# Graph layers on one core: the first load goes first, the parameters come later by GpSimd's queue, two key buffers, and a new order of all steps

## The chip, the cores and the metric

The kernel runs on one core of one Trainium2 chip. A core has TensorE (PE, matrix products; its weight loads are shown apart as PEld), VectorE (DVE), ScalarE (ACT), GpSimd (POOL) and SyncE (SP). Each works through its own list of instructions in order; semaphores let one wait for another. SP, ACT and POOL also issue DMA transfers, each from its own list, so that a DMA stands in line behind whatever its engine waits for. Time is device microseconds of one launch, the median of several runs.

## The reference, cut to what matters

Sixteen graphs (batches) of 1024 nodes with 64 channels go through four layers. Each is followed by an addition of its input and a norm over the channels. `adj` is 16 x 1024 x 1024 float32, with some ten entries in a row.

```python
# layer 0
x = ln(x + adj @ (x @ W0) + bias0)
# layer 1: Chebyshev, three products with adj
z1 = adj @ x; z2 = 2 * adj @ z1 - x; z3 = 2 * adj @ z2 - z1
x = ln(x + x @ th[0] + z1 @ th[1] + z2 @ th[2] + z3 @ th[3])
# layer 2: per node a weighted sum of quantiles (0.25, 0.5, 0.75) over its neighbours
nb = thinned(adj > 0, nodemask)          # rows with over 10 neighbours lose some
agg = weighted_quantiles(x, nb)          # a sort over a ragged list, for each channel
x = ln(x + (relu((x + agg) @ W1 + b1) @ W2 + b2) * nodemask)
# layer 3: batch norm over all batches, normalised Laplacian, leaky relu
x = ln(x + leaky((I - D^.5 A D^-.5) @ (bn(x) @ W3 + b3)))
```

## The kernel before

All 16 batches go through one software pipeline, and a last phase (lines 1640 to 1740) finishes layer 3, since its statistics run over all batches. Lines 1090 to 1640 hold a slow path for other data, which does not run here.

A batch's work is cut into nine parts, each a Python generator that gives up control at its `yield`s. The pieces between are called steps:

- `rows in` (11 steps): the x load and the first two adjacency tiles (`load`); eight tiles of 128 rows (`tile0` to `tile7`); a transpose of x; the first product with adj (`sum`). A tile's step takes the sign on ACT into `key` (L534), eight transposes on PE and two copies on ACT (`transposed`, L489, L490), the product with `keyband` on DVE (L536), eight maxima (L539), three rounds of maxima for the list (L543, L546), and issues the load of the tile after the next.
- `layers` (13): layer 0 (`part`, L570, L581), its norm (squares L440, root L443, reciprocal L445, products L450), then three hops with adj (L464) with a transpose after each, theta's product (`out`, L619), a norm, the store of the rows to DRAM for the gathers (`rows`) and x in three pieces (`parts`, L500, L502).
- `lists` (15): who is removed; nodes ordered by their number of neighbours, on PE (`before`, L724 to L728) and by eight one-hot tiles (`at0` to `at7`, L742); the ids (L765) with a comparison with caps (L775).
- `fetch` (15): 70 indirect DMAs from POOL (L803), each followed by a memset that only takes time (L806).
- `heads` (10): the gathered rows of the classes 0, 1 and 5 (24, 11 and 8 slots of 1, 4 and 3 blocks of nodes) go into the tile `home` with ACT (L875), after `dead` on DVE (L827 to L846).
- `sorts` (141): for each class a step of weights (L904), sorting steps on DVE between the tiles `home` and `away` (L907), and two or three steps of sums, products on ACT (L923) and sums on PE (L924). Class 0 has steps 0 to 84, class 1 85 to 122, class 5 123 to 140, of which 139 and 140 are sums.
- `ends` (5): the perceptron of layer 2 and its norm. `back` (11): nodes into their first order, by eight one-hot tiles (`order0` to `order7`, L988). `third` (5): adj is loaded back and multiplied once more.

No scheduler orders these: `tc.manual_schedule()` keeps the program's order. Each step has a moment in `WHEN`; batch b's step stands at b x 120 + moment, and the steps of all batches are sorted by that and written out one after the other. The moments are thus no times, only an order, the same for all engines. What an engine executes is this order, cut to its own instructions, each with its waits. Four or five batches are in work at once.

A tile name with `bufs` has so many buffers; a new tile waits for the last reader of the buffer that it gets. `key` has one, `f_a` (adjacency tiles), `at16` and `home` have two, `away` one, PSUM bank `end` one. A pool that is closed gives its memory to the next, which then waits.

Before the pipeline come the parameters (L257 to L415): loads on SP and ACT, the mask's transpose (L278), theta, W0, W2 and the biases centred on DVE, mostly in a pool `f_first` of its own that is closed ahead of the pipeline's pools. Then come keyband and columns (L1050, L1052), the memsets of the gather tiles on POOL (L1061), and the sorted steps. The loop at the end of the pipeline:

```python
        for _, b, name, u, part in sorted(parts, key=lambda p: p[0]):
            next(part)
```

## Time and profile before

| | us |
|---|---|
| median of 3 runs (2221.63 to 2226.77) | 2222.99 |
| the profiled execution, timed | 2229.29 |
| its span, first to last instruction | 2227.4 |
| first gather starts | 121.6 |
| ids of batch 0 to ids of batch 15 | 119.3 to 1940.6 |
| last phase starts | about 2147 |
| mean granted TensorE clock | 0.871 |

The profiled execution is 6.3 us above the median. The page gives busy time for each engine, slices of the span, the chain of work that ended last, groups of equal instructions with what ended the idle time before them, and DMA issues. A wait reads "engine, tile and line that waited <- what released it: total us, times, longest". A line of the timeline reads "start, length, engine, line, operation, tiles, count [idle before <- releaser]"; ACTq, SPq and POOLq are the queues' own instructions, DMA issues among them.

Where the time goes by stretches, busy us of each:

| stretch, us | DVE | ACT | PE | POOL |
|---|---|---|---|---|
| 0 to 121.6 | 83.3 | 51.6 | 85.2 | 5.0 |
| 121.6 to 243.4 | 95.1 | 62.5 | 81.0 | 109.7 |
| 243.4 to 365.1 | 111.3 | 89.4 | 96.8 | 108.1 |
| 974.0 to 1095.8 | 109.5 | 87.2 | 97.4 | 101.8 |
| 1948.1 to 2060.0 | 83.6 | 78.2 | 60.9 | 100.0 |
| 2060.0 to 2147.0 | 35.0 | 39.5 | 54.8 | 5.8 |
| 2147.0 to 2227.4 | 49.2 | 26.5 | 30.5 | 32.7 |

### The profile page before, as it was taken

The numbers are of one execution on the slowest core, as the hardware profiler recorded it, in microseconds if no ns is written. First come the engines' busy times: TensorE is split into PE (matmuls) and PEld (weight loads), VectorE is DVE, ScalarE is ACT, GpSimd is POOL, SyncE is SP. The second block draws the span as 40 slices with busy tenths as digits, with TensorE's granted clock in tenths as the row PEclk, the third lists the DMA queues.
The fourth block names the chain that finished last, engine by engine and source line by source line (L and its number), as shares of the span: only waits on it lengthen the run. The fifth ranks groups of instructions, "written<-read, shape, count | busy, mean of one in ns | idle before, by whom it ended". The sixth has DMA issues, their size and how long they took to land. (4 is left out here: it accounts for less than half of the span.)

```text
span 2227.4 us, 35713 instructions
## 1 busy us (share of the span) xinstructions
PE 1671.2 (75%) x9926; PEld 935.9 (42%) x9926; DVE 1864.1 (84%) x5687; ACT 1484.5 (67%) x5397; POOL 1734.7 (78%) x2279
## 2 busy tenths in 40 slices
PE   4876788878788778878788778878787877755653
PEld 3443444444445344444435344444444443333333
DVE  7658989889898989989898989999998988677536
ACT  3544767768686767768685767768686766675523
POOL 0078989899989989978787978889888979888014
PEclk9988889889899999989899998989998988876675
DMA  4444253533435353533535353533435352231226
GB/s 148 167 112 130 72 186 92 167 97 109 155 87 177 92 194 82 173 98 99 161 87 174 91 193 83 174 96 118 145 85 181 97 183 75 57 105 26 82 81 158
DMA packets 130481, 272.42 MB, mean 122 GB/s; under 512 B 77025, under 2 KB 77281, under 8 KB 120033
## 3 DMA queue, kind: packets, MB, share of 16 engines
q1 hardware_dynamic: 57536, 218.90, 27.2%
q0 software_dynamic: 35840, 37.92, 10.4%
q10 hardware_dynamic: 36896, 13.23, 2.4%
q8 instruction: 80, 1.31, 0.2%
q14 instruction: 129, 1.05, 0.2%
HBM read 185.89 MB, written 84.07 MB: 121 GB/s over the span
## 5 line engine op out<-in xcount | busy, mean ns | idle before, releaser
L803 POOL DMA_INDIRECT got<-rows,ids x1072 | 1139.7, 1063 | 186.0 <-issue 125.0
L806 POOL MEMSET rest<- 128x384 f32 x1120 | 509.4, 455 | 0.6
L464 PE MATMUL ps_l<-f_adj_t,f_t 128*64 128x512 f32 x1536 | 359.0, 622 | 35.5 <-ACT f_t L603 35.5
L875 ACT ACTIVATE home<-got,big 128x64 f32<-128x64 f32 x1344 | 329.9, 334 | 0.0
L907 DVE TENSOR_TENSOR away<-home 128x768 f32<-128x768 f32 (+9 forms) x416 | 228.9, 572 | 43.6 <-PE ps_xt L924 34.5
L924 PE MATMUL ps_xt<-home,quarter 128*128 128x256 f32 (+2 forms) x672 | 199.1, 404 | 65.0 <-ACT home L923 58.5
L923 ACT ACTIVATE home<-home,wts 128x64 f32<-128x64 f32 x896 | 226.8, 336 | 2.2 <-DVE home L907 2.0
L464 PEld LDWEIGHTS ps_l<-f_adj_t,f_t 128*64 128x64 f32 x1536 | 110.3, 142 | 250.7 <-issue 207.3
L539 DVE MAX8 cand<-key 128x8 f16<-128x128 f16 x1024 | 210.6, 278 | 4.4
L803 POOL DMA_INDIRECT extra<-rows,more x48 | 50.8, 1058 | 177.0 <-ACT row L780 116.1
L534 ACT ACTIVATE key<-f_a 128x1024 f16<-128x1024 f32 x128 | 135.0, 1055 | 59.2 <-DVE cand L539 42.1
L489 PE MATMUL ps_turn<-cf,f_a 128*128 128x128 f32 x1024 | 149.2, 293 | 31.2 <-ACT f_adj_t L490 18.1
L907 DVE TENSOR_TENSOR home<-away,home 128x128 f32<-128x128 f32 (+5 forms) x352 | 166.4, 473 | 6.2
L924 PEld LDWEIGHTS ps_xt<-home,quarter 128*128 128x128 f32 x672 | 110.5, 214 | 139.6 <-ACT home L923 139.5
L490 ACT COPY f_adj_t<-ps_turn 128x512 f32<-128x512 f32 x256 | 135.7, 582 | 39.3 <-PE ps_turn L489 39.3
L489 PEld LDWEIGHTS ps_turn<-cf,f_a 128*128 128x128 f32 x1024 | 120.4, 149 | 79.8 <-issue 47.6
L907 DVE TENSOR_TENSOR home<-away 128x64 f32<-128x64 f32 (+7 forms) x304 | 149.7, 510 | 1.1
L536 DVE TENSOR_TENSOR key<-key,keyband 128x1024 f16<-128x1024 f16 x128 | 87.6, 685 | 53.8 <-ACT key L534 53.8
L464 PE MATMUL ps_end<-f_adj_t,f_u 128*64 128x512 f32 x512 | 124.2, 641 | 8.9 <-ACT f_u L1015 8.9
L924 PE MATMUL ps_xt<-away,quarter 128*128 128x64 f32 (+1 forms) x448 | 94.9, 340 | 47.4 <-ACT away L923 46.8
L510 PE MATMUL ps_end<-at,f_h 128*64 128x512 f16 x256 | 62.3, 464 | 85.6 <-DVE at L988 85.5
L907 DVE TENSOR_TENSOR home<-home 128x64 f32<-128x64 f32 (+7 forms) x240 | 120.1, 500 | 7.2
(248 smaller groups left out, 3472.4 us busy)
## 6 DMA issues: line engine op xcount, KB each, us to landing
f_a<-in_adj_dram SPq DMA_DIRECT2D x128, 512.0 KB, 3.6
adj<-f_adj_t SPq DMA_DIRECT2D x16, 4096.0 KB
f_adj_t<-adj SPq DMA_DIRECT2D x64, 1024.0 KB, 22.2
got<-rows,ids POOLq DMA_INDIRECT x1072
rows<-xr ACTq DMA_DIRECT2D x16, 264.0 KB, 17.1
f_x<-in_x_dram ACTq DMA_DIRECT2D x16, 256.0 KB, 5.3
x_d<-f_x SPq DMA_DIRECT2D x16, 256.0 KB
z_d<-f_ht SPq DMA_DIRECT2D x16, 256.0 KB
```

What stands on the lines that cost most here:

```text
L464: nc.tensor.matmul(ps[h * C : (h + 1) * C, :], lhsT=v[:, j, :], rhs=pairs[:, j, h], start=(j == 0), stop=(j == NK - 1),)
L489: nc.tensor.transpose(pt[:, j * P : (j + 1) * P], a[:, (4 * g + j) * P : (4 * g + j + 1) * P], ident)
L490: nc.scalar.copy(adj_t[:, 4 * g : 4 * g + 4, i * P : (i + 1) * P], pt.rearrange("p (j n) -> p j n", n=P))
L534: nc.scalar.activation(flat_key, a, AF.Sign)
L536: nc.vector.tensor_tensor(out=flat_key, in0=flat_key, in1=keyband[:, off : off + N], op=ALU.mult)
L539: nc.vector.max(out=cand[:, i, j * 8 : j * 8 + 8], in_=key[:, j, :])
L803: nc.gpsimd.indirect_dma_start(out=w[0], out_offset=None, in_=rows[:, :], in_offset=bass.IndirectOffsetOnAxis(ap=w[1], axis=0))
L806: nc.gpsimd.memset(rest, 0.0)
L875: nc.scalar.activation(home[:, s + 1, k, :], got[:, s, k, 0:C], AF.Identity, bias=big_dead[:, s, k : k + 1], scale=1.0,)
L907: nc.vector.tensor_tensor(out=at(ho, r1 if is_max else r0, *run), in0=at(ha, r0, *run), in1=at(hb, r1, *run), op=ALU.max if is_max else AL ...
L923: nc.scalar.mul(t[:, k, :], t[:, k, :], wts[:, i, k : k + 1])
L924: nc.tensor.matmul(total, lhsT=quarter, rhs=flat(t), start=False, stop=(i == nr - 1))
```

## The change

It does four things.

- The parameters' loads leave SP's and ACT's queues and are issued by POOL, from the new function `given`, called right after batch 0's `load` step. Their working tiles are two `f_ht` buffers in place of the pool `f_first`. POOL's three memsets of the gather tiles come behind them. Keyband moves from SP's queue to ACT's, ahead of x; the columns follow x.
- Their preparation becomes a generator, `prepared`, in three pieces that run after batch 0's steps `rows in` 8 (`tile7`), `rows in` 10 (`sum`) and `layers` 1 (`square`). The arithmetic is the same, but for one subtraction that nobody used.
- `key` has two buffers.
- All moments in `WHEN` are new. In steady state this places, for example, `out` (L624 in after) between two pieces of class 5's sums and ahead of `tile6`'s transposes on PE, `perc` behind the next batch's `sum`, and the first two tiles' loads and the reload of adj some 20 to 55 earlier.

Lines behind L520 stand 5 lower in the file after; `hop2`, `norm` and `transposed` stand 74 higher.

```diff
+KEYS = 2
+SETUP = (("rows in", 8), ("rows in", 10), ("layers", 1))
...
 WHEN = {
-    "rows in": (-237, -232.5, -224.8, -221.8, -214.5, -211.4, -205.5, -203.1, -200.2, -196.4, -192.2),
-    "layers": (-156, -124.5, -120.4, -111.8, -102.1, -98.2, -94.1, -87.1, -85, -81.1, -76.5, -76.3, -70),
-    "lists": (-133.4, -133.4, -125.8, -125.8, -99.2, -69.7, -69.6, -67.8, -65.7, -63, -59.4, -58.3, -55.8, -40.9, -4.9),
-    "fetch": (-27, -9.9, -9.3, 4.7, 4.7, 4.7, 4.7, 4.7, 4.7, 26.1, 28.6, 42.7, 55.6, 64.2, 64.2),
-    "heads": (25.6, 34.3, 34.8, 84.7, 97.5, 97.5, 104.6, 135.7, 140.2, 142.2),
+    "rows in": (-291.1, -231, -226.2, -221.4, -216.1, -211.1, -203.2, -202.1, -200.7, -195.1, -189.8),
+    "layers": (-161.4, -122.7, -116.3, -107.2, -103.4, -100.5, -94.9, -86.6, -82.5, -82.1, -77.1, -70.1, -68),
+    "lists": (-136.1, -134.1, -134, -126.8, -94.1, -66.3, -64.9, -63.8, -53.4, -53.2, -50.1, -43.3, -41.9, -15.3, -4.7),
+    "fetch": (-2.9, -2.9, -0.1, 7.1, 18.4, 20.7, 29.9, 29.9, 29.9, 29.9, 29.9, 30.5, 30.6, 36, 48.7),
+    "heads": (24.2, 36.5, 36.6, 89.8, 104.8, 107.1, 109.7, 129.4, 134.3, 140.7),
     "sorts": (
...
-        146.7, 147, 147, 147, 147, 147, 148.1, 148.2, 154.7, 155.6, 155.6, 155.6, 156.2, 156.9, 157.4, 158.8,
+        156, 156, 156, 156, 157.9, 158.8,
     ),
-    "ends": (159.7, 161.1, 161.2, 173.5, 185.2),
-    "back": (137.4, 189.4, 195.6, 202.6, 202.7, 206.9, 209.5, 215.7, 220.2, 220.2, 224.2),
-    "third": (212.3, 228.2, 241.9, 249.6, 264.9),
+    "ends": (164.6, 169.7, 171.2, 175.2, 199.2),
+    "back": (140.7, 166.9, 200.2, 202.8, 208.3, 208.3, 212.8, 215, 217, 221.7, 226.5),
+    "third": (190.8, 233.1, 244.7, 252.9, 270.2),
...
+    def given(pw):
+        one, two = (pw.tile([P, 512], F32, name="f_ht", bufs=2) for _ in range(2))
...
+        for h in range(2):
+            nc.gpsimd.dma_start(out=w0_c[h * C : (h + 1) * C, 0, :], in_=w0)
+        nc.gpsimd.dma_start(out=left[:, 0, :], in_=bias0.rearrange("(o c) -> o c", o=1).to_broadcast([3, C]))
+        nc.gpsimd.dma_start(out=left[:, 1, :], in_=b2.rearrange("(o c) -> o c", o=1).to_broadcast([3, C]))
+        nc.gpsimd.dma_start(out=mask_u, in_=nodemask.rearrange("b (k p) -> (b k) p", p=P))
+        nc.gpsimd.dma_start(out=th, in_=theta.rearrange("k i o -> i k o"))
+        nc.gpsimd.dma_start(out=w2_s, in_=w2)
+        for h in range(2):
+            nc.gpsimd.dma_start(out=w1_2[h * C : (h + 1) * C], in_=w1)
+        nc.gpsimd.dma_start(out=b1_s, in_=b1.rearrange("(h o) -> h o", o=1))
+        return th, thp, mean, w0_c, left, mine, term
...
+    def prepared(th, thp, mean, w0_c, left, mine, term):
+        halves = [slice(h * C, (h + 1) * C) for h in range(2)]
+        centred(mean, w0_c)
...
+        nc.vector.tensor_copy(out=biases, in_=mine)
+        yield
+        nc.vector.tensor_copy(out=mask_f, in_=mask_u)
+        pm = bank("end")
+        nc.tensor.transpose(pm[:, 0:P], mask_f, ident)
+        nc.vector.tensor_copy(out=mask_t, in_=pm[:, 0:P])
+        nc.vector.tensor_copy(out=earlier, in_=earlier_f)
...
+        centred(mean, thp)
+        thf = bank("end").rearrange("p (k c) -> p k c", c=C)[:, 0:4]
+        nc.tensor.matmul(thf, lhsT=but_last, rhs=thp, start=True, stop=True)
+        for hp in halves:
+            nc.vector.tensor_copy(out=th_c[hp, :, hp], in_=thf[hp])
+        yield
+        nc.vector.tensor_copy(out=w2_c[:, 0, :], in_=w2_s)
+        centred(mean, w2_c)
+        nc.vector.tensor_scalar(out=node, in0=own, scalar1=-1.0, scalar2=None, op0=ALU.add)
+        nc.scalar.mul(quarter, ident, 0.25)
+        nc.scalar.mul(minus_i, ident, -1.0)
+        yield
...
-            key = pa.tile([P, NK, P], F16, name="key")
+            key = pa.tile([P, NK, P], F16, name="key", bufs=KEYS)
...
-        nc.sync.dma_start(out=keyband, in_=ch_d[:, 5 * P : 5 * P + BAND])
+        nc.scalar.dma_start(out=keyband, in_=ch_d[:, 5 * P : 5 * P + BAND])
...
+        def setup():
+            nc.scalar.dma_start(out=columns, in_=ch_d[:, 5 * P + BAND : 6 * P + BAND + N])
+            todo = prepared(*given(pw))
+            for ns, _, _, ks in CLASSES:
+                if any(WHOLE[k] < ns for k in ks):
+                    nc.gpsimd.memset(gots[ks[0]], 0.0)
+            nc.vector.tensor_copy(out=rec[:, :, OTHERS], in_=own)
+            for u in SETUP:
+                then[0, *u] = lambda: next(todo)
...
+        then = {(0, "rows in", 0): setup}
         for _, b, name, u, part in sorted(parts, key=lambda p: p[0]):
             next(part)
+            if (b, name, u) in then:
+                then[b, name, u]()
```

## The prediction

> **What bounds the kernel now.** I read the busy times first, then five windows of 126 us, then VectorE's waits, then the timeline of the first 125 us and of one cycle.

> ```profile
> span 2227.4 us, 35713 instructions
> PE 1671.2 (75%) x9926; PEld 935.9 (42%) x9926; DVE 1864.1 (84%) x5687; ACT 1484.5 (67%) x5397; POOL 1734.7 (78%) x2279
> ...
> 804.00:930.00 126.00, 99.42 (x623) 55.61 (x620) 113.88 (x355) 92.52 (x339) 109.35 (x144) 0.93 0.45 136
> ...
> L765 ACT CAST ids<-ps_l x16: 312/318/318, 119.3 to 1940.6; 128x184 int32<-128x184 f32 x16
> ```

> VectorE (DVE) is busiest, with 113.9 of a cycle's 126 us, and GpSimd (POOL) follows with 109.4. The window's columns are length, PE, PE weight loads, DVE, ACT, POOL. The list of ids is made once a batch: 15 steps from 119.3 to 1940.6 are 121.4 us each. In single rows it is made for batch 1 at 209.3 and for batch 14 at 1825.42, so the 13 cycles between take 124.3 each. A batch's 70 gathers need some 70 x (1063 + 455 + 160) ns = 117.5 us of POOL (mean gather, mean memset, the pause that the rows show), so POOL is not the bound; it waits for ids and rows. What separates DVE from a full cycle is this (300 to 1800 us, 12 cycles):

> ```profile
> DVE key L536 <- ACT key L534: 21.5, 12, 2.4
> DVE x_mid L500 <- ACT f_h L450: 20.8, 10, 2.1
> DVE at L988 <- PE ps_end L510: 18.7, 28, 1.9
> DVE away L907 <- PE ps_xt L924: 12.2, 12, 1.0
> DVE n_r L445 <- ACT n_d L443: 4.2, 10, 0.4
> DVE x_mid L500 <- issue: 4.2, 2, 2.1
> ```

> Per cycle: 1.8 for the sign key, 2.1 for x_mid, 1.6 for order tiles, 1.0 for the first sort step, 0.4 for a root: 6.9 us. The rest of the idle time is pauses of some 0.05 us. So at most 6.9 us a cycle can be won by another order. The start is the other place:

> ```profile
> 15.59 0.33 SPq L1050 DMA_DIRECT2D keyband<-in_ch_dram  x1
> ...
> 15.96 24.99 SPq L481 DMA_DIRECT2D f_a<-in_adj_dram  x8
> ...
> 21.25 1.06 ACT L534 ACTIVATE key<-f_a 128x1024 f16<-128x1024 f32 x1 [16.36 <-DMA f_a<-in_adj_dram]
> ...
> 47.57 9.05 PE L464 MATMUL ps_l<-f_adj_t,f_x 128*64 128x512 f32 x32
> ...
> 61.72 1.28 ACT L443 ACT_TABLE_LOAD   x1
> ```

> The first adjacency load is issued at 15.96, when the parameters are done (their pool's memory is used again), and its sign runs at 21.25.

> **The start, step by step.** The load now stands second on SP, behind cf (issued at 0.76), so at some 1.2 us; with the same 5.3 us to its sign this runs near 6.5, say 6.8: 14.4 us earlier. Keyband and x go by ACT's own queue, in front of the sign, and have landed by then as x does before. Eight DVE tiles take 3.70 each before (23.06 to 26.76) and have no gap, so a second key buffer gives nothing here; they end 14.4 earlier.

> Then part is given back. In times of before, less 14.4: DVE ends tile 7 at 51.95; the first piece of preparation (L443 to L467) repeats rows that span 11.07 to 15.52, with the centres 4.6 us: 56.5, while PE's hop runs to 56.6. But in PE's new order the mask transpose and theta's product (L472, L487) stand between hop and layer 0's product (L575). Mask cast, transpose 0.48, copy 0.29, then DVE's casts and eight theta steps, 2.5: the product starts at 60.1, takes 1.2, and layer 0's product ends at 63.7 instead of 58.9. DVE goes on with theta's copies (0.9), the whole lists (51.95 to 60.4 before: 8.5), w2's centring (1.0) and only then reaches the reciprocal of layer 0: 72.0 instead of 63.5. So 8.5 is lost and 5.9 remains. In batch 0's layers the out product (L624) now stands ahead of tile 6's transposes on PE, so that tile's copies, the next sign and the squares of the second norm come later: the rows above give 2.3, and 0.4 for the hop behind. The lists of batch 1 now start before the cap comparison that waited 2.0 us. Net: -5.9 + 2.7 - 2.0 = -5 us. From 178 us on DVE is saturated and passes this on. Bounds: -14.4 if all is hidden, +3 if POOL's loads are late.

> Ten small loads move from ACT's and SP's queues to POOL, ahead of its three memsets (4.79 us). At 1.06 us each (a gather's row) they are issued by 12 us and the memsets by 17. Needed first is w0 at 37.5. The first gather comes past 115. Cover: 20 us; without it a us late is a us lost. A row shows what POOL's memsets do to DVE copies:

> ```profile
> 0.75 4.79 POOL L1061 MEMSET got<- 128x1518 f32 x3 [0.29 <-POOLq L1751]
> ...
> 3.41 2.18 DVE L379 COPY w_c<-w_s 128x64 f32<-128x64 f32 x1 [1.41 <-DMA w_s<-in_L_gnn_W_dram]
> ```

> That copy ends with the memset (5.59 against 5.54). In after the memsets fall on tiles, which are tensor_tensor and max, not copies, so I charge 0.

> [...]

> **The cycle, step by step.** I laid the after order of each engine beside the rows of one cycle and asked which wait must remain.
> - Sign key, 1.8: with two buffers the sign waits for no max. From `dead5`, for which ACT waits, ACT has 13.3 us of work to `dead0` and DVE 22.3: a lead of 9. From there to tile 5's sign ACT has 21.7 and DVE 16.4: 5.3 of the lead are used. 0 (high 1.8).
> - First sort step, 1.0: it must wait until the old away buffer is read. Before, 21 products of class 5 (5.1 us) run after the last step and DVE hides 3.9 of it in tile 6. Now PE's order is three sums, out product, tile 6's transposes, four sums; ACT's is nine products, sign 6, tile 6's copies, twelve products. Chain after the last step: 2.2 + 0.3 + 3.7 (L619) + 1.05 + 0.6 + 2.2 + 1.1 = 11.1; less 0.5 for ranks ready early. DVE has two tiles and the weights between, 7.6. So 3.0 (low 2.8; high 5.4 with ACT as late as the 2.4 us seen at the key).
> - x_mid behind eight ACT products in one step: unchanged, 2.1.
> - Order tiles: spread between sort steps, 1.6 becomes 0 (high 1.6). Root: ten sort steps instead of six cover it, 0 (high 0.4).
> - New: `perc` now stands behind the next batch's hop on PE (7.7 mean, 8.4 in this cycle), then 2.4 and ACT's eight, 1.8; DVE's addition comes 9 us after the root: 0.5 (0 to 3).
> - New: class 1 starts when its last 16 home copies (3.9) are done, behind ten products (2.4); lists cover all but 1.0 (0 to 3).

> Sum 3.0 + 2.1 + 0.5 + 1.0 = 6.6 against 6.9: -0.3, times 13 is -4. All low ends give 4.9, -2.0 a cycle; all high ones 17.3, but a wait gives ACT and PE a lead for the next, so I stop at 9.5: +2.6 a cycle.

> **The end.** Ids of batch 14 start the last two rounds of gathers; beside DVE's cycle they come 0 to 2 us later, and in the last batch class 5's start stands earlier among the steps: 0 in all (+-5).

> Sum: -5 - 4 = -9: span 2218.4, and 2220.3 timed, as the profiled execution took 2229.29. That is 6.3 above the median of the runs, 2222.99; put against the median the forecast is 2223 - 9 = 2214.

> **Rivals.**
> 1. *The sums wait* (slower). First sort step and class 1 both meet their high ends; the place is PE's out product ahead of the four sums. For it: ACT is busy 92 of 126 us and its 1.8 us lateness at the key is exactly in this stretch. Against: ACT has no max to wait for. Price: +2.4 + 2.0 - 0.3 = +4.1, eased to +2 a cycle, 13 x 2 - 5 = +21: 2244. It decides from +0.8 a cycle.
> 2. *The order works as drawn*: only x_mid stays, -4.8 a cycle. -62 - 5: some 2156; POOL's 117.5 is then just not reached. For it: no wait but the 2.1 is forced by data alone. Against: the 11.1 us chain.
> 3. *The first load does not do what it says*: all 14.4 is given back, since layer 0 needs what was moved behind it; the cycle gives -4: 2219.

> **How the numbers follow.** Chances: forecast 0.50 (own range 2200 to 2226), first rival 0.24, second 0.16, third 0.10. About 0.2%, 4.4 us, is what a measurement of this kernel can tell from no change. Of the forecast's 0.50 I count 0.35 faster, 0.13 same, 0.02 slower; of the third 0.05, 0.03, 0.02. Faster 0.56, same 0.16, slower 0.28. The range cuts the fast end of rival 2 and takes in most of rival 1: 2182 to 2242.

> **What would show it.** First sign near 6.8 us; layer 0's reciprocal at 57 to 58; first gather near 118. In mid cycle a wait of some 3 us at the first sort step for ps_xt, none for the key, and cycles of ids at 124 us. It is wrong if the first sort step waits over 4 us, if DVE waits for got (gathers late), if cycles fall below 121, or if the reciprocal already comes at 50.

## The result and the profile after

| | before | after |
|---|---|---|
| median, us (4 runs each) | 2222.31 (2220.84 to 2226.77) | 2285.98 (2284.47 to 2287.2) |
| ratio after to before, 95% interval | | 1.028 (1.0261 to 1.0299) |
| span of the profiled execution | 2227.4 | 2285.2 |
| mean granted TensorE clock | 0.871 | 0.831 |

The kernel became slower by 2.8%; forecast were 2214 us and a range up to 2242. The ids of each batch split the 57.8 us between the spans:

| stretch | before | after | difference |
|---|---|---|---|
| start to the ids of batch 1 | 209.3 | 200.2 | -9.1 |
| 13 cycles, ids of batch 1 to ids of batch 14 | 1616.1 | 1677.6 | +61.5 |
| ids of batch 14 to ids of batch 15 | 115.2 | 112.3 | -2.9 |
| ids of batch 15 to the end | 286.8 | 295.1 | +8.3 |

So the start won time, the end gave 5.4 back in all, and the cycle lost 4.7 us, 13 times. The page of after begins:

```profile
span 2285.2 us, 35621 instructions
...
PE 1753.8 (77%) x9926; PEld 989.9 (43%) x9926; DVE 1861.3 (81%) x5686; ACT 1486.0 (65%) x5397; POOL 1749.6 (77%) x2289
```

VectorE's work is the same (1861.3 against 1864.1). TensorE runs the same 9926 products and needs 82.6 us more for them (1753.8 against 1671.2): its instructions became longer. VectorE's waits of after, 300 to 1800 us, which holds 11 to 12 cycles:

```profile
DVE away L912 <- PE ps_xt L929: 46.6, 11, 4.5
DVE x_mid L505 <- ACT f_h L376: 25.0, 12, 2.1
DVE f_h L966 <- issue: 21.6, 8, 3.1
DVE n_r L371 <- ACT n_d L369: 13.6, 20, 1.2
DVE f_h L966 <- ACT f_h L965: 9.9, 4, 2.9
DVE at L747 <- PE ps_px L515: 6.7, 11, 0.7
DVE key L541 <- ACT key L539: 4.1, 9, 1.6
```

The key's wait is nearly gone, but per cycle the first sort step now waits 4.2 us, the perceptron's addition f_h 2.7, x_mid 2.1, the root 1.2, a one-hot tile 0.6, the key 0.3: 11.1 in place of before's 6.6 (both over the ten cycles from the fourth to the fourteenth ids, waits of over 0.25 us each). Nearly all but x_mid lies in one stretch of some 35 us, from the last sums of class 5 to f_h. TensorE's rows there, in one cycle of after:

```profile
1311.25 0.59 PE L929 MATMUL ps_xt<-away,quarter 128*128 128x192 f32 x2 [1.93 <-DVE wts L909]
1311.97 1.73 PE L929 MATMUL ps_xt<-home,quarter 128*128 128x192 f32 x4
1313.49 4.91 PE L624 MATMUL ps_l<-th_c,f_ct 128*128 128x128 f32 x32
1318.24 1.04 PE L415 MATMUL ps_turn<-cf,f_a 128*128 128x128 f32 x8
1320.72 0.59 PE L929 MATMUL ps_xt<-away,quarter 128*128 128x192 f32 x2 [1.44 <-ACT away L928]
...
1329.37 0.94 PE L402 MATMUL ps_xt<-cf,f_ht 128*128 128x128 f32 x4 [2.10 <-ACT f_ht L937]
...
1332.99 8.78 PE L390 MATMUL ps_l<-f_adj_t,f_x 128*64 128x512 f32 x32
```

The out product takes 4.91 us and the hop 8.78. The same two in the same stretch of before:

```profile
1299.07 4.13 PE L619 MATMUL ps_l<-th_c,f_ct 128*128 128x128 f32 x32
...
1309.92 7.09 PE L464 MATMUL ps_l<-f_adj_t,f_x 128*64 128x512 f32 x32
```

Over the ten cycles from the fourth ids to the fourteenth, the out product takes 4.80 on average in after and 4.01 in before, the hop 8.75 and 7.67. The prediction took 3.7 for the out product, as rows of before with the full clock have it (those that start at 98.67 and 921.21 us). The windows of the stretch in after show why; they are cut on the raster of 3.41 us on which the clock's changes lie (last section; columns as in the prediction: length, PE, weight loads, DVE, ACT, POOL, granted clock, DMA share, GB/s):

```profile
1305.71:1309.12 3.41, 3.41 (x18) 1.08 (x14) 3.27 (x6) 3.41 (x12) 3.08 (x5) 1.00 0.10 20
1309.12:1312.54 3.42, 1.37 (x6) 0.60 (x4) 3.28 (x11) 3.42 (x13) 3.09 (x5) 1.00 0.55 176
1312.54:1315.95 3.41, 3.29 (x15) 3.27 (x15) 3.20 (x15) 1.04 (x2) 3.08 (x5) 0.50 0.19 22
1315.95:1319.36 3.41, 3.33 (x30) 3.09 (x29) 2.50 (x14) 0.48 (x2) 3.08 (x5) 1.00 0.19 19
1319.36:1322.78 3.42, 1.78 (x6) 0.89 (x6) 0.01 (x1) 3.42 (x15) 3.09 (x6) 1.00 0.12 21
1322.78:1326.19 3.41, 3.33 (x14) 3.24 (x15) 3.29 (x10) 2.14 (x5) 3.08 (x5) 0.50 0.11 20
1326.19:1329.60 3.41, 1.31 (x12) 1.12 (x11) 3.23 (x10) 3.19 (x19) 3.08 (x5) 1.00 0.89 356
1329.60:1333.02 3.42, 2.75 (x10) 0.84 (x8) 3.32 (x7) 1.27 (x3) 3.09 (x5) 0.50 1.04 425
1333.02:1336.43 3.41, 3.41 (x10) 0.97 (x10) 2.30 (x7) 3.07 (x11) 2.95 (x5) 0.50 1.46 477
```

Read it line against line: here a window in which PE was busy 1.37, 1.78 or 1.31 of 3.41 us is followed by one at half clock, whatever then runs in it. What runs in them is the out product, the last sums with tile 7's transposes, the perceptron and the hop's beginning. The same stretch before has one such window, ahead of the sums; the hop and nearly all of the out product run at full clock after it (rows as above, the last one is the hop's):

```profile
1289.64:1293.06 3.42, 1.32 (x10) 1.03 (x10) 3.18 (x12) 3.42 (x9) 3.09 (x5) 1.00 0.35 50
1293.06:1296.47 3.41, 2.49 (x7) 1.85 (x8) 3.27 (x15) 3.41 (x16) 3.08 (x5) 0.50 0.19 20
1296.47:1299.88 3.41, 3.41 (x12) 2.77 (x12) 2.28 (x8) 2.31 (x10) 3.08 (x5) 0.50 0.14 20
1299.88:1303.30 3.42, 3.42 (x33) 3.42 (x32) 3.35 (x6) 0.98 (x2) 3.09 (x5) 1.00 0.10 20
...
1310.12:1313.54 3.42, 3.42 (x18) 1.14 (x16) 3.28 (x9) 1.00 (x5) 3.09 (x5) 1.00 1.09 451
```

### The profile page after: what moved, and what is told of

Read it like the earlier page. It is cut to its first block, busy times and chain, and to the rows that moved or that the text cites. A ratio compares the mean times of both kernels' runs of the same rounds, so it can differ in the third digit from the quotient of the medians.

```text
span 2285.2 us, 35621 instructions
## 1 busy us (share of the span) xinstructions
PE 1753.8 (77%) x9926; PEld 989.9 (43%) x9926; DVE 1861.3 (81%) x5686; ACT 1486.0 (65%) x5397; POOL 1749.6 (77%) x2289
## 3 DMA queue, kind: packets, MB, share of 16 engines
q8 instruction: 80, 1.31, 0.2%
## 5 line engine op out<-in xcount | busy, mean ns | idle before, releaser
L390 PE MATMUL ps_l<-f_adj_t,f_t 128*64 128x512 f32 x1536 | 342.1, 598 | 0.7 <-ACT f_t L608 0.7
L929 PE MATMUL ps_xt<-home,quarter 128*128 128x256 f32 (+2 forms) x672 | 211.2, 424 | 85.5 <-ACT home L928 57.8
L544 DVE MAX8 cand<-key 128x8 f16<-128x128 f16 x1024 | 210.6, 278 | 4.4
L929 PEld LDWEIGHTS ps_xt<-home,quarter 128*128 128x128 f32 x672 | 122.6, 239 | 163.8 <-ACT home L928 126.2
L415 PE MATMUL ps_turn<-cf,f_a 128*128 128x128 f32 x1024 | 158.5, 305 | 21.0 <-DMA f_a<-in_adj_dram 13.0
L415 PEld LDWEIGHTS ps_turn<-cf,f_a 128*128 128x128 f32 x1024 | 130.0, 157 | 66.2 <-issue 24.9
L390 PE MATMUL ps_end<-f_adj_t,f_u 128*64 128x512 f32 x512 | 137.0, 695 | 8.2 <-ACT f_u L1020 8.2
L929 PE MATMUL ps_xt<-away,quarter 128*128 128x64 f32 (+1 forms) x448 | 101.1, 363 | 53.1 <-ACT away L928 49.3
L539 ACT ACTIVATE key<-f_a 128x1024 f16<-128x1024 f32 x128 | 136.0, 1063 | 8.3 <-DMA f_a<-in_adj_dram 6.1
L390 PE MATMUL ps_l<-f_adj_t,f_x 128*64 128x512 f32 x512 | 136.3, 688 | 0.0
```

Source lines behind the costliest of these rows:

```text
L390: nc.tensor.matmul(ps[h * C : (h + 1) * C, :], lhsT=v[:, j, :], rhs=pairs[:, j, h], start=(j == 0), stop=(j == NK - 1),)
L415: nc.tensor.transpose(pt[:, j * P : (j + 1) * P], a[:, (4 * g + j) * P : (4 * g + j + 1) * P], ident)
L539: nc.scalar.activation(flat_key, a, AF.Sign)
L544: nc.vector.max(out=cand[:, i, j * 8 : j * 8 + 8], in_=key[:, j, :])
L929: nc.tensor.matmul(total, lhsT=quarter, rhs=flat(t), start=False, stop=(i == nr - 1))
```

## The experiments

Three questions: which part of the change costs the time, whether waits of this stretch may be added up, and what the clock has to do with it. In the table, cycle and waits (of over 0.25 us each) are means of the ten cycles from the fourth ids to the fourteenth in the profiled execution, half clock is the time in a cycle at a granted clock of 0.50, from the trace's record of the clock, and the ratio is to before on the same chip.

| run | median us | ratio, interval | cycle us | DVE waits us | half clock us |
|---|---|---|---|---|---|
| before | 2222 to 2228 | | 124.9 | 6.6 | 22.5 |
| after | 2285.98 | 1.0261 to 1.0299 | 129.6 | 11.1 | 37.2 |
| old_moments | 2217.82 | 0.9943 to 0.9984 | 125.2 | 7.1 | 23.6 |
| keys_one | 2217.86 | 0.9963 to 1.0004 | 124.3 | 6.3 | 21.8 |
| out_behind | 2278.91 | 1.021 to 1.0297 | 129.7 | 11.1 | 36.9 |
| perc_first | 2295.42 | 1.03 to 1.0359 | 129.5 | 11.0 | 37.2 |
| both_moved | 2245.5 | 1.0068 to 1.013 | 126.2 | 7.9 | 31.1 |
| warm | 2253.39 (one run) | | 127.0 | 8.1 | 29.4 |
| warm_elsewhere | 2288.32 | 1.027 to 1.0309 | 129.7 | 11.1 | 32.4 |
| warm_more | 2221.32 | 0.9977 to 1.0006 | 124.4 | 5.5 | 20.8 |
| before_warm | 2228.58 | 0.999 to 1.0041 | 125.3 | 7.0 | 22.5 |
| stretch | 2238.24 | 1.0051 to 1.0115 | 125.9 | 7.6 | 29.0 |
| split | 2212.08 | 0.9944 to 0.9983 | 123.9 | 5.7 | 28.3 |
| root_first | 2199.96 | 0.9871 to 0.9917 | 122.8 | 4.0 | 25.9 |
| root_warm | 2196.45 | 0.9854 to 0.9896 | 122.9 | 4.1 | 22.9 |
| at_later | 2188.0 | 0.9829 to 0.9861 | 123.0 | 4.6 | 28.8 |
| at_later_filled | 2197.4 | 0.983 to 0.99 | 122.7 | 4.1 | 23.1 |

**Which part.** old_moments: the changed kernel with before's `WHEN`.

```diff
-    "rows in": (-291.1, -231, -226.2, ...
+    "rows in": (-237, -232.5, -224.8, ...
...
```

> The changed kernel with the moments of before; the early load, the parameters by GpSimd and two key buffers stay. Theory A (the new order costs it): cycles of ids back to 125 or, as the key's wait of 1.8 a cycle falls, to 123.3; with 5 to 9 us won at the start 2191 to 2217. Rival B (the second key buffer or the new start slows the cycle): near 2286, cycles near 129.7.

It is 0.4% faster than before, by what the start gives: its ids of batch 1 come at 200.9 against 209.3, and its 13 cycles take 1617.2 against 1616.1. The new order alone costs the time. But the key's wait stayed, at 1.9 us a cycle, with two buffers. keys_one asks whether the buffer does anything:

```diff
-KEYS = 2
+KEYS = 1
```

> The early start with the moments of before (run old_moments) and one key buffer instead of two. In old_moments the wait for the key stayed at 1.9 us a cycle with two buffers. Theory A (the sign is late because it stands behind other work in ACT's list): 2218 +- 4, wait 1.9 as before. Rival B (the second buffer does help elsewhere): slower by 5 or more.

2217.86 against 2217.82: with before's order the second buffer gives nothing that can be told. In old_moments the late sign stands in ACT's list behind class 5's products and a copy that waits 1.10 us for TensorE's sums (the cycle at 1284.85 us). What the buffer does in the new order no run asks; there the signs of tiles 4 and 6 start 5.2 and 0.8 us before the maxima of the tile ahead end, which one buffer would not allow.

**Whether waits add up.** Three edits of after's moments; in perc_first row1 moves too, for it shares the PSUM bank `end` with the perceptron.

```diff
 out_behind, both_moved:
-    "layers": (... -86.6, -82.5, -82.1, -77.1, ...
+    "layers": (... -86.6, -82.5, -81.1, -77.1, ...
 perc_first, both_moved:
-    "ends": (164.6, 169.7, 171.2, 175.2, 199.2),
-    "back": (140.7, 166.9, ...
+    "ends": (158.95, 161.1, 161.2, 175.2, 199.2),
+    "back": (140.7, 158.85, ...
```

> The changed kernel with the out product behind the last sums of class 5 instead of ahead of them. Theory A1 (each wait stands alone): the 4.2 us at the first sort step become about 1.0, 13 x 3.1 = -40: 2246. Theory A2 (a chain through PE and ACT runs from these sums to the perceptron's addition, and a wait taken away comes back at the next link): the wait moves to the root n_r and to f_h, 0 to -10: 2276 to 2286. Rival C (the lower clock of TensorE makes the time, whatever the order): cycles stay at 129.7.

> The changed kernel with the perceptron of layer 2 (summed, hidden, perc, and row1 whose PSUM bank it shares) ahead of the next batch's norm and hop, as before; the out product stays ahead of the last sums. A1: the waits for f_h (2.6 a cycle) and n_r (1.1) go, 13 x 3.7 = -48: 2238. A2: nearly the same, -42: 2244, with the first sort step still waiting 4.2. C: 2286.

> Both moves together. A1: -88: 2198. A2: only when both are moved does the chain get short; some 5.7 a cycle, -74: 2212, cycles near 124. C: 2286.

The waits of out_behind, same view and stretch as for after:

```profile
DVE n_r L371 <- ACT n_d L369: 56.3, 12, 5.3
DVE x_mid L505 <- ACT f_h L376: 25.0, 12, 2.1
DVE f_h L966 <- ACT f_h L965: 22.3, 9, 2.7
...
DVE away L912 <- PE ps_xt L929: 5.6, 8, 0.9
```

The first sort step lost 41 us of waiting (46.6 to 5.6) and the root gained 43 (13.6 to 56.3). The sum a cycle is 11.1 as in after. The links (sums, out, tile 7, squares, xn, perceptron, root) run through ACT and TensorE one after the other and were only put in another order. In perc_first the wait turned up at a third place, where theories A1 and A2 expected 42 to 48 us less:

```profile
DVE key L541 <- ACT key L539: 41.3, 17, 3.6
DVE away L912 <- PE ps_xt L929: 36.4, 11, 4.5
```

There tile 7's sign stands in ACT's list behind the copy of row1, which waits 2.80 us for TensorE (the cycle at 1325 us), and xn, and both come after the late sums. The cycle stayed as in after (129.5 against 129.6); the 9 us by which perc_first is slower lie behind the ids of batch 14. Only both_moved shortens the chain, and by 3.4 us a cycle, not by the 5.7 expected: the key still waits 4.6. Waits of this chain don't add up. That three orders have nearly the same cycle could have a second reason, the raster of the clock (last section), which these runs don't tell apart from the chain.

**What the clock does.** warm adds transposes of the identity where TensorE pauses, into a PSUM bank that is free at this time; nobody reads them. warm_elsewhere, its control, adds as many behind `tile2` and `tile4`, where TensorE is busy.

```diff
             next(part)
+            if (name, u) in (("rows in", 7), ("back", 1)):
+                spare = bank("px")
+                for _ in range(8):
+                    nc.tensor.transpose(spare[:, 0:P], ident, ident)
 warm_elsewhere:
+            if (name, u) in (("rows in", 3), ("rows in", 5)):
 warm_more:
+            more = {("layers", 8): 12, ("rows in", 7): 8, ("rows in", 8): 8, ("back", 1): 8}
```

> The changed kernel with 16 added transposes of the identity a cycle, into a PSUM bank that nobody reads, 8 behind tile 6's transposes and 8 behind row1, where TensorE waits 1.4 and 2.1 us. Theory C (idle pauses lower the granted clock there, and slow products stretch the chain): the clock of this stretch rises, the hop falls from 8.8 to about 7.1, cycles fall to 127 to 128.5: 2245 to 2270. Theory A2 (the chain is made of waits between ACT and TensorE, the clock is a by-product): cycles stay at 129.7 or grow by up to 2: 2286 to 2310.

> The control for warm: the changed kernel with the same 16 transposes a cycle, but behind the transposes of tiles 2 and 4, where TensorE is busy and has its full clock already. Theory C (they help only where TensorE pauses): cycles stay at 129.7 or grow, 2286 to 2310. Rival (the added instructions help by a side effect, as a shift of phases): near 2253.

> The changed kernel with 36 transposes of the identity a cycle instead of warm's 16: 12 behind the hop sum3, 8 behind tile 6's transposes, 8 behind tile 7's, 8 behind row1, so that TensorE hardly pauses from sum3 to the next hop. Theory C1 (the clock makes all of the loss against before): cycles 124.5 to 125.5 and 2215 to 2235. Theory C2 (the clock makes the 2.6 that warm won, the length of the chain at full clock the rest): cycles 126.5 to 128, 2245 to 2265, as warm. If the filling itself delays the chain: above 128.

More work on TensorE made the kernel faster: 2253 with 16 transposes a cycle in the pauses (one run), 2221 with 36, and 2288 with 16 outside of them. warm holds both cases side by side. In four of its ten cycles the out product kept the full clock, in six it didn't:

```profile
1042.23 3.73 PE L624 MATMUL ps_l<-th_c,f_ct 128*128 128x128 f32 x32
1050.34 0.96 DVE L912 TENSOR_TENSOR away<-home 128x768 f32<-128x768 f32 x1 [2.91 <-PE ps_xt L929]
...
1170.31 4.85 PE L624 MATMUL ps_l<-th_c,f_ct 128*128 128x128 f32 x32
1179.53 0.96 DVE L912 TENSOR_TENSOR away<-home 128x768 f32<-128x768 f32 x1 [4.33 <-PE ps_xt L929]
```

The four waits of the first sort step are 2.6 to 3.0 us, the six 4.1 to 4.5. The control is not neutral, though: in warm_elsewhere the half clock falls by 4.8 us a cycle too, and the out product takes 3.73 in all ten cycles. But ACT's products of class 5 start there 1.7 us later against VectorE than in after, presumably behind the added work, so the first sort step still waits 3.9; the perceptron's first products and the hop's beginning stay at half clock, and the cycle keeps its length. It shows that added transposes don't help by themselves, and that this one product's clock isn't enough.

The rows and windows of warm_more in the stretch:

```profile
1277.00 3.73 PE L624 MATMUL ps_l<-th_c,f_ct 128*128 128x128 f32 x32
1280.57 1.04 PE L415 MATMUL ps_turn<-cf,f_a 128*128 128x128 f32 x8
1281.44 1.04 PE L1096 MATMUL ps_px<-cf 128*128 128x128 f32 x8
```

```profile
1272.74:1276.15 3.41, 2.63 (x18) 2.04 (x18) 3.27 (x9) 3.41 (x12) 3.08 (x5) 1.00 0.51 174
1276.15:1279.57 3.42, 3.30 (x28) 3.00 (x27) 3.21 (x16) 1.31 (x3) 3.09 (x5) 1.00 0.18 28
1279.57:1282.98 3.41, 2.91 (x27) 2.67 (x25) 2.81 (x15) 1.77 (x6) 3.08 (x5) 1.00 0.20 19
...
1293.22:1296.63 3.41, 3.41 (x18) 1.13 (x17) 3.34 (x10) 2.02 (x7) 3.08 (x5) 1.00 1.16 481
```

In every window of the stretch PE is now busy 1.9 us or more, and none is at half clock. The out product takes 3.73 us, and the mean hop product of the next batch falls from 704 to 595 ns. What is left of the waits:

```profile
DVE away L912 <- PE ps_xt L929: 32.5, 12, 2.9
DVE x_mid L505 <- ACT f_h L376: 25.0, 12, 2.1
DVE key L541 <- ACT key L539: 7.1, 7, 1.6
...
DVE f_h L966 <- ACT f_h L965: 1.5, 1, 1.5
DVE n_r L371 <- ACT n_d L369: 1.4, 8, 0.2
```

f_h and the root no longer wait, the first sort step waits 2.7. This is theory C1: the clock made all of the loss of the cycle. (No run sets it by itself; filled pauses, with warm's two kinds of cycle and the control beside them, are how it is shown. The 36 transposes have no control of their own.) 13 cycles of warm_more take 1611.9 us, 4.2 less than before's. The end's loss is another matter: from the ids of batch 14 on before takes 402.0 us, after 407.4 and warm_more 409.2.

before_warm puts 12 such transposes behind before's tile 6.

> The kernel before with 12 transposes of the identity behind tile 6's, where TensorE waits 3.0 us and the clock of the next 5 us is 0.50. Theory C: class 5's sums take 3.5 in place of 5.3 and the 1.0 us at the first sort step goes; the later links keep their clock: -13, 2210. If that wait is not on the chain: 2223.

No difference that can be told: the wait at the first sort step fell from 1.0 to 0.9 only, and the half clock stayed at 22.5 us a cycle, so the filling did not reach what it was meant for.

**A better order.** From after's order, with the early start; each run keeps the edits of the one above it.

```diff
 stretch: tile6 -202.4, sum -187; out -82.3, square2 -80;
          ends (159.5, 161.1, 161.2, 172.9, 199.2); row1 158.85
 split:
         yield from norm(pw, x3p, [h], "n2", centred=True)
+        yield "x3p root"
         st.update(x3p=in_three(pw, x3p, "x3"))
          ends (159.5, 161.1, 161.2, 172.9, 193.5, 199.2)
 root_first: turned -187.05; square2 -78.7
 at_later: at1 -62.85, at2 -59.85
 root_warm, at_later_filled: 12 and 14 transposes of the identity behind tile7
```

> The changed kernel with one stretch in another order: tile 6 and the out product ahead of class 5's sums, then the sums, row1, tile 7 with its sign ahead of summed, square2, hidden, perc; the addition f_h ahead of the next batch's hop in ACT's list, the hop behind it. A2: worked out along the rows of the changed kernel, the sums end at some 1318.6 where DVE reaches its first sort step at 1318.6, and the root and f_h come in time: the waits of the stretch fall from 8.5 to under 1.5, x_mid's 2.1 stays, cycles 121.5 to 123: 2180 to 2205. If another chain or GpSimd (117.5 a cycle) takes over: 124 to 126, 2212 to 2240.

> As stretch, and the step x3p cut in two: the root and the products go five sort steps and two tiles earlier than x_mid, so that DVE doesn't wait 2.1 for ACT's eight products. A2: 2.1 a cycle less than stretch, 16 x 2.1 = -33, as long as GpSimd's 117.5 is not reached. If DVE isn't what bounds the cycle any more: the same time as stretch.

> As split, and in ACT's list the perceptron's relu ahead of the norm's squares, and the root n_d and its products ahead of the copy f_x0t, for which it stood 4.6 us in split while TensorE worked at half clock. Theory A2: the wait for n_r, 3.6 a cycle in split, goes; cycles 120 to 121 and 13 x 3.6 less: 2155 to 2170 where split was 2203 to 2212. If the wait comes back at f_h or GpSimd (117.5 a cycle, plus its waits for ids) takes over: 122 to 124, 2185 to 2212.

> As root_first, with 12 transposes of the identity behind tile 7's, where TensorE waits 2.2 us and the clock then fell to 0.50 in split. Theory C: hop and perceptron at full clock, another 0 to 2 us a cycle, up to -25; if DVE no longer waits in this stretch: the same time as root_first.

> root_first with the one-hot tiles at1 and at2 some 3 and 3 sort steps later, as the second and third of them waited 2.2 us a cycle for TensorE there, which does the hop first. A2 (waits of DVE): 2.2 a cycle less, 13 x 2.2 = -29: 2171. Theory D (a cycle holds a whole number of the clock's 3.413 us steps: 38 in the changed kernel, 37 in both_moved, 36 in root_first): the cycle stays at 122.8 or drops to 35 x 3.413 = 119.5; 2200 or 2157.

> at_later with 14 transposes of the identity behind tile 7's, where TensorE pauses 2.2 us and the clock then is 0.50 through the perceptron and most of the hop (10.2 us). Theory C: perceptron and hop at full clock, the waits of the one-hot tiles behind them (1.0 a cycle at at1 to at7, some of the 3.1 in all) go: cycles 121 to 122, 2165 to 2180. If the pauses of the reordering behind it, or the rest of DVE, decide: 2185 to 2195.

stretch missed its 2180 to 2205: its root waits 3.6 us, since n_d stands on ACT behind a copy (f_x0t) that waits 4.55 us for a perceptron and a transpose at half clock. split won 26 us by hiding x_mid's wait, and root_first 12 more. at_later, at 2188.0, is 1.55% faster than before (ratio 0.9845, 0.9829 to 0.9861) and beats both kernels. How its two moves won the time isn't shown: its profiled execution took 2196.43, the other three 2186.93 to 2188.05, and it has the cycle of root_first's. Against root_first's, the wait at the tiles at0 to at7 falls from 1.9 to 0.9 us a cycle, and at the order tiles one of 2.2 comes in place of 0.3: a wait came back at the next link once more. Filling pauses no longer helped in these orders, though the half clock fell (25.9 to 22.9 and 28.8 to 23.1 us a cycle): root_warm against root_first is 3.5 us apart, at_later_filled 9.4 above at_later, with overlapping intervals. Nor does the half clock of a whole cycle tell the time: split and at_later are faster than before with 28.3 and 28.8 us against 22.5. Which products it meets seems to count. Why at_later is the fastest of them is open.

## Why the prediction was wrong

- **The start**: right in its mechanism, too small in size. The first sign came at 6.55 (forecast 6.8), layer 0's reciprocal at 56.7 (57 to 58), the first gather at 115.2 (118). The ids of batch 1 came 9.1 us earlier where -5 was forecast. GpSimd's small loads took 0.52 to 0.68 us each and its memsets ended at 13.8, hidden as forecast. Beside the memsets the tile's product with keyband took 0.67 us and its eight maxima 1.65 (L541 at 11.37, L544 at 12.07), and the same behind them (15.07, 15.78), so the 0 charged there holds. The third rival, that the saving is all given back, fell with old_moments.
- **The key**: the wait went, from 1.8 to 0.3. Whether by the second buffer, as the prediction put it, is open: in before's order it gives nothing (keys_one), in the new one it is used, but no run leaves it out.
- **The cycle, its durations**: the step that failed. The chain to the first sort step was priced as "2.2 + 0.3 + 3.7 (L619) + 1.05 + 0.6 + 2.2 + 1.1", with the out product as it ran at full clock. In after it took 4.91, 1.2 us more, and the wait was 4.2 where 3.0 was forecast. At full clock the chain was priced rightly: from the start of its weights to the first sort step are 10.2 to 10.6 us in warm's four cycles with the full clock, against the forecast's 10.6, and 11.8 to 12.1 in its other six. For f_h the hop was taken at 7.7 with the perceptron behind it; the hop took 8.78 and started behind the perceptron's first products at half clock; f_h waited 2.7 where 0.5 was forecast. The root, "0 (high 0.4)", became 1.2. With the pauses filled the same three are 2.7, 0.1 and 0.1, and the 13 cycles are 4.2 us shorter than before's. The forecast said 4; that the two agree so well is partly luck, as 5.5 us of waits are left and not its 6.6. The prediction laid the new order beside rows of the old one and never asked at which clock the products would run in the new one, though the profile of before showed a case of it: the window of 1.32 busy us is followed by a clock of 0.50.
- **The cycle, its cap**: "a wait gives ACT and PE a lead for the next, so I stop at 9.5". Measured are 11.1. In out_behind a wait of this chain gives no lead; the next link is late too. The first rival had one of the places, and its price before easing (+4.1, measured +4.7) was near by luck: its two terms, +2.4 at the first sort step and +2.0 at class 1, are +1.2 and -1.0 in after, and the rest came from f_h and the root. Eased to +2 it read 2244.
- **The other terms**: x_mid stayed at 2.1 as forecast; class 1's start, put at 1.0, doesn't wait; the order tiles went to 0 as forecast, but the tiles at0 to at7, for which the sum has no term, wait 0.6.
- **The end**: 0 with 5 either way; it was +5.4, and no run separates why.

## What to carry to other kernels

When an order is changed, look at the pauses it gives TensorE, not only at who waits for whom. In after, windows of 3.41 us in which PE was busy 1.31 to 1.78 us were followed by a clock of 0.50, and the out product, on a chain between engines, took 4.91 us in place of 3.7. Price a chain of waits as one length: in out_behind the first sort step waited 41 us less and the root, further along the chain, 43 more. Where a pause can't be removed, products that nobody reads can be put into it: in warm_more they were worth 65 us out of 2286, in three other orders (before_warm, root_warm, at_later_filled) nothing. A control that puts them elsewhere shows whether it is the pause that counts, if one also looks at what it does to the clock.
